# A block-diagonal spectrum stored with the frequency innermost: contiguous evictions, strided weight loads

## Chip, cores, metric

One core of one Trainium2 chip. The metric is device time in microseconds (us) of one execution. The granted clock is the share of TensorE's full clock that the throttle granted, as the profile records it. The experiments ran on two chips on which the kernel before takes about 7346 us instead of the 7284 of the result (whose chip is not on record); so experiments are compared by their ratio to the kernel before in the same rounds.

## The reference, cut to what matters

```python
def reference(x, conv_weight, ty, tx, pole1, pole2, residue):   # x: 16 x 16 x 256 x 256, fp32
    x = x + conv3x3(gn(x), conv_weight)          # circular convolution
    v = gn(x)
    alpha = fft2(v)                              # over rows, then columns
    S = einsum('ikpq,oikp,xikq->oxik', residue, A, Bm)     # a 16 x 16 matrix per frequency
    r1 = einsum('biox,oxik->bkox', alpha, S)     # mixing of channels at each frequency
    return x + ifft2(r1).real + transient(alpha, pole1, pole2, residue)
```

All arithmetic is fp32. The kernel writes the transforms as matmuls and uses that the input is real: 129 of 256 rows of the spectrum, in 33 groups of four rows (the last has one).

## The kernel before

Stage 2 works through the 33 groups. For each it transforms the rows along x (`forward`), copies the result out of PSUM into the block-diagonal tile `abd` (such a copy is called an eviction), makes the mixing matrices (`weights`, into `sg`), mixes (`mix`), and transforms back (`backward`). The parts that the change and the argument touch:

```python
    px = p2.enter_context(tc.tile_pool(name="p_x", bufs=2, space=PSUM))
    ...
    # Normalised spectrum, block diagonal in the group's rows: [(s, i, ri), fx, (s', b)]
    abd = big.tile([P, N, SB], FP, name="abd", tag="abd")        # P=128, N=256, SB=64
    ...
    def forward(g):
            ...
            for b in range(0, BQ, 2):
                ps = px.tile([P, 2, N], FP, name="ps_x", tag="ps_x")
                ... 8 fp32 matmuls into ps[:m, bb]                                # L556
                for s in range(nf):
                    rows = slice(32 * s, 32 * s + 32)
                    at = s * B + b0 + b
                    o = abd[rows, :, at : at + 2].rearrange("p n b -> p b n")
                    if s % 2:
                        nc.scalar.copy(o, ps[rows])                               # L569
                    else:
                        nc.vector.tensor_copy(o, ps[rows])                        # L571
    def weights(g):
            ...   # L629 matmuls into ps_s; copies into sg, L638 (DVE) and L640 (ACT)
            o = sg[:m, :, 2 * k : 2 * k + 2].rearrange("p n r -> p r n")
    def mix(g):
        for f0 in range(0, P, 16):
            ps = pm.tile([P, 16, 2 * C], FP, name="ps_mix", tag="ps_mix")
            for j in range(16):
                for xc in range(2):
                    f = xc * P + f0 + j
                    nc.tensor.matmul(                                             # L656
                        ps[64 * xc : 64 * xc + r, j],
                        lhsT=abd[:m, f, :r],
                        rhs=sg[:m, f],
                        start=True, stop=True)
    def backward(g):
            ...   # transposes L684 of yt[:, :, 2 * k + ro], matmuls L700, copies
```

The two values of `xc` write partitions 0 and 64, and in the trace their matmuls start in pairs, some 7 ns apart; I call them the two column halves of the array. An fp32 matmul of the mixing is recorded as two matmul instructions, each with its own weight load (in the 32 full groups, 8192 matmuls as 16384 of each), so the 256 frequencies of a group are 512 loads of 64 columns.

Of the kernel before, what the change touches and what calls it, by code (L numbers as in the profile page):

```python
# [10 lines left out]
FP = mybir.dt.float32  # L11
# [4 lines left out]
DRAM = bass.MemoryType.DRAM  # L16

C = 16  # channels, in and out
N = 256  # image side
P = 128  # L20
NT = 43  # blocks of 6 output rows; the last one starts at row 250
NPAIR = 22
NFY = 129  # rows of the half spectrum
PAD = 1024  # floats between the groups of a DRAM scratch, off a pitch of a power of two
# [4 lines left out]
def conv_then_laplace_kernel(ctx: ExitStack, tc: tile.TileContext, a: dict, out: bass.AP):  # L29
    """x1 = x + conv3x3(gn(x)); out = x1 + laplace(gn(x1)).  # L30

    1a  per image: group norm of x, the circular 3x3 convolution with the residual in its centre
        tap, statistics of the sum v; beside it the tables that depend on poles and residues
    1b  per image: gn(v), its Fourier transform along y, and its projections on the poles
    2   per 4 rows of the half spectrum: transform along x, mixing of channels per frequency,
        transform back along x
    3   per image: transform back along y, plus the transient part, plus v
    """
# [13 lines left out]
    tabs = cp.tile([P, 2, 2, N], FP, name="tabs", tag="tabs")  # cos | sin, row halves, columns  # L52
# [12 lines left out]
    # Rows padded by 64, which keeps its pitch off a power of two.  # L65
# [4 lines left out]
    # omega = 2 pi k / (n d), for the columns k of krow etc.  # L70
# [6 lines left out]
    rd = cp.tile([P, 2], FP, name="rd", tag="rd")  # 1 / (n d), along y and along x  # L77
# [8 lines left out]
    vmr = tp.tile([P, 2, B, C], FP, name="vmr", tag="vmr")  # 1/std and -mean/std of v  # L86
# [3 lines left out]
    # ---------------------------------------------------------------- 1a  # L90
# [25 lines left out]
    def sqrt_eps(sd, var, eps, tmp):  # L116
        """sd = sqrt(var + eps), var overwritten with var + eps; one Newton step."""
        nc.vector.tensor_scalar(var, var, eps, None, ALU.add)
        nc.scalar.activation(sd, var, AF.Sqrt)
        nc.vector.reciprocal(tmp, sd)  # L120
        nc.vector.tensor_tensor(tmp, tmp, var, ALU.mult)
        nc.vector.tensor_tensor(sd, sd, tmp, ALU.add)
        nc.vector.tensor_scalar(sd, sd, 0.5, None, ALU.mult)

    def group_sums(st, n, wt, gmat, tag):
        """Weighted sums over a partition's rows: of values, the group mean, of squares about it."""
        f = st.rearrange("p t (h s) -> p t h s", s=3)
        mean, m2 = f[:, :, :, 1], f[:, :, :, 2]
        tmp = sp.tile([P, NPAIR, 2], FP, name=f"tmp{tag}", tag=f"tmp{tag}")[:n]
        dev = sp.tile([P, NPAIR, 2], FP, name=f"dev{tag}", tag=f"dev{tag}")[:n]  # L130
        s = sp.tile([P, 4], FP, name=f"sum{tag}", tag=f"sum{tag}")[:n]
        nc.vector.tensor_tensor(tmp, mean, wt[:, 0], ALU.mult)
        nc.vector.tensor_reduce(s[:, 0:1], tmp, AX.XY, ALU.add)
        ps = pst.tile([P, 32], FP, name="ps_stat", tag="ps_stat")
        nc.tensor.matmul(ps[:n, 0:1], lhsT=gmat, rhs=s[:, 0:1], start=True, stop=True)
        nc.vector.tensor_copy(s[:, 1:2], ps[:n, 0:1])
        nc.vector.tensor_scalar(dev, mean, s[:, 1:2], None, ALU.subtract)
        nc.vector.tensor_tensor(dev, dev, dev, ALU.mult)
        nc.vector.tensor_tensor(dev, dev, wt[:, 0], ALU.mult)
        nc.vector.tensor_tensor(tmp, m2, wt[:, 1], ALU.mult)  # L140
        nc.vector.tensor_tensor(tmp, tmp, dev, ALU.add)
        nc.vector.tensor_reduce(s[:, 2:3], tmp, AX.XY, ALU.add)
        return s
# [83 lines left out]
    # Tables of the poles and residues, in steps between the images.  # L227
    def make_hat(side):
        """hat[t, i, (k, p, ri)]: transform of 1 / (i omega - pole) from frequencies to places."""
# [6 lines left out]
        for cc in (slice(0, n // 2), slice(n // 2, n)):  # L236
            pb = sw.tile([P, n // 2, 2], FP, name="s_pb", tag="s_a")
            nc.sync.dma_start(out=pb, in_=a[f"pole{side + 1}"][cc].partition_broadcast(P))
            for h in range(2):
                w, r = im[h][:, cc], re[h][:, cc]  # L240
                den = sw.tile([P, n // 2], FP, name="s_den", tag="s_b")
                nc.vector.tensor_scalar(w, pb[:, :, 1], -1.0, kcol[:, h : h + 1], ALU.mult, ALU.add)
                nc.gpsimd.tensor_tensor(den, w, w, ALU.mult)
                nc.gpsimd.tensor_tensor(r, pb[:, :, 0], pb[:, :, 0], ALU.mult)
                nc.gpsimd.tensor_tensor(den, den, r, ALU.add)
                nc.vector.reciprocal(den, den)
                # minus the real part, and the imaginary part
                nc.gpsimd.tensor_tensor(r, pb[:, :, 0], den, ALU.mult)
                nc.vector.scalar_tensor_tensor(w, w, -1.0, den, ALU.mult, ALU.mult)
# [4 lines left out]
        for yc in range(2):  # L254
            yy = slice(yc * P, yc * P + P)
            for half in range(2):
                cc = slice(half * 512, half * 512 + 512)
                for ri in range(2):
                    ps = psu.tile([P, 512], FP, name="ps_setup", tag="ps_setup")
                    for h in range(2):  # L260
                        # re: cos Re + sin Im;  im: cos Im - sin Re
                        first, second = ((neg, im), (im, re))[ri]
                        nc.tensor.matmul(
                            ps, lhsT=cosT[:, h, yy], rhs=first[h][:, cc], start=h == 0, stop=False
                        )
                        nc.tensor.matmul(
                            ps, lhsT=sinT[:, h, yy], rhs=second[h][:, cc], start=False, stop=h == 1
                        )
                    nc.scalar.copy(hv[:, yc, cc, ri], ps)

    def make_coef():
        """coef[(k, q, r), i, (k', p, s)]: what the products of parts r and s count in the residue
        sum's real and imaginary part, zero unless k = k'."""
# [17 lines left out]
    def make_exps(which):  # L291
        """e[(.., ri), i, t] = exp(pole t), for the poles along y with the imaginary part negated."""
# [30 lines left out]
    def make_c_start():  # L323
        """c[(i, p, ri), set, k, x]: sum over q of residue / (i omega - pole2) / 2, and in set 1 the
        conjugate of the same at -x."""
# [69 lines left out]
    # ---------------------------------------------------------------- 1b  # L395
# [15 lines left out]
    for b in range(B):  # L411
# [71 lines left out]
        # rows re: (re, im) of the sum; rows im: (-im, re)  # L483
# [9 lines left out]
    # ---------------------------------------------------------------- 2  # L493
# [19 lines left out]
    pimS = kp.tile([P, 2, C], FP, name="pimS", tag="pimS")  # imaginary parts, and conjugated  # L513
# [4 lines left out]
    # minus the real parts, on the rows re and on the rows im  # L518
# [5 lines left out]
    # Normalised spectrum, block diagonal in the group's rows: [(s, i, ri), fx, (s', b)]  # L524
    abd = big.tile([P, N, SB], FP, name="abd", tag="abd")
# [5 lines left out]
    def forward(g):  # L531
        """Transform of the group's rows along x into abd."""
        nf = 4 if g < 32 else 1
        m = nf * 32
        for b0 in range(0, B, BQ):
# [14 lines left out]
            for b in range(0, BQ, 2):  # L550
# [13 lines left out]
                for s in range(nf):  # L564
                    rows = slice(32 * s, 32 * s + 32)
                    at = s * B + b0 + b
                    o = abd[rows, :, at : at + 2].rearrange("p n b -> p b n")
# [5 lines left out]
    def weights(g):  # L573
        """s[(s, i, ri), fx, (k, ro)]: the channels' mixing at the group's frequencies."""
# [8 lines left out]
        for st in range(2):  # L583
# [9 lines left out]
            # rows re: Re and Im of 1 / (i omega - pole1); rows im: -Im and Re  # L593
# [49 lines left out]
    def mix(g):  # L643
        """y[(fx half, s, b), fx, (k, ro)] = sum over i."""
# [6 lines left out]
# [4 lines that stand above are left out]
# [3 lines left out]
                        lhsT=abd[:m, f, :r],  # L658
# [13 lines left out]
    def backward(g):  # L672
        """Transform back along x, into wD."""
# [3 lines left out]
        for k0 in range(0, C, 4):  # L677
            wo = wop.tile([P, 4, N], FP, name="wo", tag="wo")
            for k1 in range(0, 4, 2):
                # [fx, k, fx half, ro, (s, b)]  # L680
# [6 lines left out]
                # (re, im), and (-im, re) for the sines  # L687
# [24 lines left out]
            for ro in range(2):  # L712
                # The imaginary parts of rows 0 and 128 count nothing: row 128 takes that place.
# [22 lines left out]
    # ---------------------------------------------------------------- 3  # L736
# [51 lines left out]
def _constants():  # L788
    """Tables that depend on shapes alone."""
# [56 lines left out]
def _laid_out(x, L0_conv_weight, L1_conv_ty, L1_conv_tx, L1_conv_weights_pole1, L1_conv_weights_pole2, L1_conv_weights_residue):  # L846
    """The inputs in the layouts that the program reads."""
    g = {"x": np.asarray(x), "ty": np.asarray(L1_conv_ty), "tx": np.asarray(L1_conv_tx)}
    w = np.asarray(L0_conv_weight)  # co, ci, 3, 3
    band = np.zeros((8, C, 3, 6, C), w.dtype)  # L850
    for yo in range(6):
        for jy in range(3):
            # out row yo takes in row yo + 2 - jy of the block with its halo
            band[yo + 2 - jy, :, :, yo, :] = w[:, :, jy, :].transpose(1, 2, 0)
# [11 lines left out]
    # (k, q, r), i, p  # L866
    g["res_kq"] = np.repeat(rs.transpose(1, 3, 0, 2, 4).reshape(64, C, 4, 2), 2, 0)
    # (i, p, r), k, q
# [3 lines left out]
    # (r, c, p), i and (c, q, r), i  # L872
# [20 lines left out]
```

## Time and profile before

| | before |
|---|---|
| time, median of 4 | 7283.7 us (7280.2 to 7292.5) |
| mean granted TensorE clock | 0.938 |
| stage 2, first L556 to last L700 | 3727 us |
| mixing L656, start to start | 29.2 ns per instruction, 58.4 ns per pair of halves |
| recorded wait of ps_x (L556) on the ACT copy | 98.9 us |

The rows of the groups are quoted in the prediction below. They read: line, engine, operation, target and sources, number of instructions, then busy time in us and mean ns of one, then the idle time of the engine just before them and who ended it.

### The profile page before, as it was taken

What the parts mean: (1) busy time and instruction counts of PE and PEld (TensorE: products, weight loads), DVE (VectorE), ACT (ScalarE), POOL (GpSimd) and SP (SyncE); (2) the same over time, 40 slices, a digit from 0 to 9 for tenths busy, and PEclk for the clock granted to TensorE, in tenths of its full rate; (3) what the DMA queues carried; (4) which work ended last, traced back from release to release, by engine and by line L of the source; (5) the groups of instructions that cost most, each with busy time, mean ns of one, the idle gap of its engine ahead of it and who ended that gap; (6) DMA issues with size and microseconds to landing.
All of it is one profiled execution on the core that took longest, in us unless ns stands there. A gap on an engine that the chain in (4) does not pass through costs nothing.

```text
span 7295.4 us, 99265 instructions
## 1 busy us (share of the span) xinstructions
PE 6262.9 (86%) x41824; PEld 4914.9 (67%) x41824; DVE 2863.8 (39%) x5620; ACT 1845.7 (25%) x2602; POOL 984.8 (13%) x1259
## 2 busy tenths in 40 slices
PE   4876777786776776999999999999999999999999
PEld 1322222266666665888888888888888888868888
DVE  3576666433333334343333433433334334322222
ACT  2233223211111112232232332322323323211111
POOL 1211111000000002121221211212112112100000
PEclk9988888898888888999999999999999999999999
DMA  8677777746656653111111111111111111137777
GB/s 108 100 123 120 117 113 119 112 106 111 110 104 109 111 93 81 34 36 44 36 39 39 36 44 36 36 43 34 42 38 36 44 33 39 27 127 261 262 262 235
DMA packets 459980, 655.84 MB, mean 90 GB/s; under 512 B 34576, under 2 KB 347920, under 8 KB 459152
## 3 DMA queue, kind: packets, MB, share of 16 engines
q1 hardware_dynamic: 359184, 470.16, 31.0%
q0 software_dynamic: 32768, 112.21, 7.7%
q10 hardware_dynamic: 67584, 67.12, 2.6%
q8 instruction: 331, 5.42, 0.3%
q14 instruction: 113, 0.93, 0.0%
HBM read 372.05 MB, written 277.35 MB: 89 GB/s over the span
## 4 chain that ended last, share of the span: by engine, by line
PE 65%; DMA 13%; DVE 11%; ACT 5%; SPq 4%; issue 1%; POOL 1%; ACTq 0%; DVEq 0%; POOLq 0%
PE ps_inv L700 13%; PE ps_s L629 10%; PE ps_x L556 8%; PE ps_mix L656 7%; PE ps_conv L191 5%; PE ps_dft L434 5%; DMA xt<-in_x 4%; DMA x1nD<-gat 4%; ACT abd L569 3%; DVE abd L571 3%; PE ps_f L778 3%; PE ps_f L777 3%; PE ps_f L776 3%; DMA vD<-vt 3%; PE ps_dft L442 3%; SPq L470 2%
## 5 line engine op out<-in xcount | busy, mean ns | idle before, releaser
L556 PE MATMUL ps_x<-tabs,t 128*128 128x256 f32 (+1 forms) x4224 | 980.7, 385 | 141.0 <-ACT abd L569 98.9
L700 PE MATMUL ps_inv<-tabs,tr 128*128 128x256 f32 (+1 forms) x4224 | 1043.2, 400 | 16.9 <-DVE tr L694 11.7
L191 PE MATMUL ps_conv<-xt,wband 128*96 128x512 f32 (+1 forms) x1408 | 712.0, 623 | 302.6 <-ACT vt L198 278.5
L556 PEld LDWEIGHTS ps_x<-tabs,t 128*128 128x128 f32 (+1 forms) x4224 | 767.8, 188 | 294.1 <-ACT abd L569 140.5
L629 PE MATMUL ps_s<-ct,ab 128*128 128x256 f32 (+1 forms) x4224 | 929.5, 380 | 9.6 <-ACT sg L640 9.6
L700 PEld LDWEIGHTS ps_inv<-tabs,tr 128*128 128x128 f32 (+1 forms) x4224 | 800.9, 195 | 179.9 <-ACT tr L692 41.0
L629 PEld LDWEIGHTS ps_s<-ct,ab 128*128 128x128 f32 (+1 forms) x4224 | 789.2, 188 | 140.0 <-issue 21.2
L571 DVE COPY abd<-ps_x 32x512 f32<-32x512 f32 x520 | 535.4, 1030 | 434.7 <-ACT abd L569 241.5
L191 PEld LDWEIGHTS ps_conv<-xt,wband 128*96 128x96 f32 x1408 | 238.6, 174 | 683.8 <-issue 360.8
L569 ACT COPY abd<-ps_x 32x512 f32<-32x512 f32 x512 | 529.5, 1034 | 578.6 <-DVE abd L571 576.1
L656 PE MATMUL ps_mix<-sg,abd 128*64 128x32 f32 (+1 forms) x16896 | 540.9, 223 | 61.3 <-DVE sg L638 59.3
L613 POOL TENSOR_TENSOR ab<-uv,kmask 128x512 f32<-128x512 f32 x512 | 542.6, 1061 | 357.9 <-PE ps_s L629 313.5
L656 PEld LDWEIGHTS ps_mix<-sg,abd 128*64 128x64 f32 (+1 forms) x16896 | 515.4, 137 | 111.4 <-DVE sg L638 62.6
L434 PE MATMUL ps_dft<-fy,vy 128*128 128x258 f32 x2048 | 562.6, 399 | 8.5 <-DVE vy L421 8.5
L454 PE MATMUL psd<-gs,hat 128*128 128x128 f32 x1024 | 225.0, 311 | 305.3 <-DVE gs L452 305.3
L638 DVE COPY sg<-ps_s 128x512 f32<-128x512 f32 (+1 forms) x264 | 273.7, 1037 | 496.4 <-PE ps_s L629 495.5
L548 POOL COPY t<-t 128x256 f32<-128x256 f32 (+1 forms) x264 | 111.1, 453 | 2571.7 <-PE ps_x L556 2105.8
L449 ACT COPY gat<-ps_dft 128x258 f32<-128x258 f32 x512 | 195.2, 384 | 1033.0 <-PE ps_dft L442 758.1
L198 ACT ACTIVATE vt<-ps_conv,sumx 96x512 f32<-96x512 f32 x352 | 224.1, 670 | 772.5 <-DMA vD<-vt 418.4
L640 ACT COPY sg<-ps_s 128x512 f32<-128x512 f32 (+1 forms) x264 | 277.5, 1051 | 541.1 <-PE ps_s L629 540.3
L779 DVE TENSOR_TENSOR ol<-ps_f,vl 128x512 f32<-128x512 f32 x256 | 176.9, 692 | 601.6 <-PE ps_f L778 595.0
L454 PEld LDWEIGHTS psd<-gs,hat 128*128 128x128 f32 x1024 | 175.3, 209 | 341.7 <-DVE gs L452 324.0
(177 smaller groups left out, 6848.6 us busy)
## 6 DMA issues: line engine op xcount, KB each, us to landing
vy<-vD SPq DMA_DIRECT2D x128, 512.0 KB, 5.6
x1D<-gat SPq DMA_DIRECT2D x32, 2048.0 KB, 25.0
t<-x1D SPq DMA_DIRECT2D x256, 256.0 KB, 3.3
wl<-wD SPq DMA_DIRECT2D x128, 512.0 KB, 4.8
vl<-vD POOLq DMA_DIRECT2D x128, 512.0 KB, 8.1
out_y<-ol ACTq DMA_DIRECT2D x128, 512.0 KB, 9.1
wD<-wo SPq DMA_DIRECT2D x252, 256.0 KB, 3.2
vD<-vt SPq DMA_DIRECT2D x80, 768.0 KB, 4.7
```

The lines of the kernel that those rows point to most:

```text
L191: nc.tensor.matmul(ps[:, :m], lhsT=wc if tap == 1 else wband[:, tap, :], rhs=t[:, t0 + j : t0 + j + m, 2 - tap : 2 - tap + N], start=tap == 0,
L434: nc.tensor.matmul(ps[:, 0 : 2 * NFY], lhsT=vy[:, h, j, xx], rhs=fy[:, h], start=h == 0, stop=h == 1,)
L454: nc.tensor.matmul(psd[:, j], lhsT=hat[1][:, xc, i], rhs=gs[:, xc], start=xc == 0, stop=xc == 1)
L556: nc.tensor.matmul(ps[:m, bb], lhsT=t[:, xc, b + bb, :m], rhs=tab[:, xc], start=n == 0, stop=n == 3,)
L569: nc.scalar.copy(o, ps[rows])
L571: nc.vector.tensor_copy(o, ps[rows])
L613: nc.gpsimd.tensor_tensor(ab.rearrange("p a s i r -> p (a s) i r"), uv[:, k].rearrange("p t o s r -> p (t o s) r").unsqueeze(2).to_broadca ...
L629: nc.tensor.matmul(ps[:m, ro], lhsT=ab[:, 2 * st + ro, :nf].rearrange("p s i r -> p (s i r)"), rhs=ct[:, st, k], start=st == 0, stop=st == 1,)
L638: nc.vector.tensor_copy(o, ps[:m])
L640: nc.scalar.copy(o, ps[:m])
L656: nc.tensor.matmul(ps[64 * xc : 64 * xc + r, j], lhsT=abd[:m, f, :r], rhs=sg[:m, f], start=True, stop=True,)
L700: nc.tensor.matmul(ps[: 2 * r, kk], lhsT=t[:, kk, xc], rhs=tab[:, xc], start=n == 0, stop=n == 3,)
```

## The change

The intent: write `abd` with the frequency innermost, so that an eviction writes 256 contiguous floats per image instead of single floats 256 bytes apart. The price: the 64 weight columns of a mixing matmul are then 1024 bytes apart. Comments were dropped as well, which changes nothing that runs.

```diff
-    # Normalised spectrum, block diagonal in the group's rows: [(s, i, ri), fx, (s', b)]
-    abd = big.tile([P, N, SB], FP, name="abd", tag="abd")
+    abd = big.tile([P, SB, N], FP, name="abd", tag="abd")
...
-                    o = abd[rows, :, at : at + 2].rearrange("p n b -> p b n")
+                    o = abd[rows, at : at + 2]
...
-                        lhsT=abd[:m, f, :r],
+                        lhsT=abd[:m, :r, f],
```

## The prediction

> **What bounds the kernel now.** I read the page first, for the stretch in which the changed tile lives. The changed tile, abd, exists only in stage 2 (33 groups: transform along x, mixing, transform back).
>
> ```profile
> PE 6262.9 (86%) x41824; PEld 4914.9 (67%) x41824; DVE 2863.8 (39%) x5620; ACT 1845.7 (25%) x2602; POOL 984.8 (13%) x1259
> ...
> PE   4876777786776776999999999999999999999999
> ```
>
> From about slice 16 on TensorE is at 90% or more. Starts of L569 in the trace put stage 2 from about 2770 to 6470 us, one full group every 110.6 us; in the window 2760 to 6475 us TensorE is busy 3503.6 of 3715 us, DVE 1412.7, ACT 1097.4. So DVE and ACT seconds are nearly free here; only what holds TensorE counts.
>
> Next, the groups that touch abd, and the waits list for TensorE:
>
> ```profile
> L571 DVE COPY abd<-ps_x 32x512 f32<-32x512 f32 x520 | 535.4, 1030 | 434.7 <-ACT abd L569 241.5
> ...
> L569 ACT COPY abd<-ps_x 32x512 f32<-32x512 f32 x512 | 529.5, 1034 | 578.6 <-DVE abd L571 576.1
> L656 PE MATMUL ps_mix<-sg,abd 128*64 128x32 f32 (+1 forms) x16896 | 540.9, 223 | 61.3 <-DVE sg L638 59.3
> ```
>
> ```profile
> PE ps_x L556 <- ACT abd L569: 98.9, 96, 2.9
> ```
>
> The evictions of ps_x cost 535 + 530 us of DVE and ACT, but TensorE stands still for them only 98.9 us in the whole run. The timeline of one group shows how:
>
> ```profile
> 4344.55 7.17 PE L556 MATMUL ps_x<-tabs,t 128*128 128x256 f32 x32 [1.34 <-ACT abd L569]
> ...
> 4348.31 1.03 DVE L571 COPY abd<-ps_x 32x512 f32<-32x512 f32 x1 [1.69 <-PE ps_x L556]
> 4349.37 1.02 ACT L569 COPY abd<-ps_x 32x512 f32<-32x512 f32 x1 [1.68 <-DVE abd L571]
> 4350.42 1.02 DVE L571 COPY abd<-ps_x 32x512 f32<-32x512 f32 x1 [1.09 <-ACT abd L569]
> ...
> 4351.48 1.04 ACT L569 COPY abd<-ps_x 32x512 f32<-32x512 f32 x1 [1.09 <-DVE abd L571]
> ...
> 4352.58 0.70 PE L556 MATMUL ps_x<-tabs,t 128*128 128x256 f32 x2 [0.86 <-ACT abd L569]
> ```
>
> The four evictions of one ps_x tile run strictly one after another, DVE, ACT, DVE, ACT, 4.2 us from 4348.31 to 4352.52. There are two ps_x buffers. A tile is 16 matmul instructions at 216 ns (start to start) = 3.46 us. The third tile needs the first tile's buffer, so each two tiles cost TensorE 0.86 us of standing.
>
> [...] The kernel before writes abd with 256 bytes between neighbouring elements[...] the copies of wo, which have the same shape and a contiguous target, take 679 and 575 ns instead of 1030 and 1034.
>
> ```profile
> L709 DVE COPY wo<-ps_inv 32x512 f32<-32x512 f32 x4 | 2.7, 679 | 13.4 <-PE ps_inv L700 13.4
> ...
> L711 ACT COPY wo<-ps_inv 32x512 f32<-32x512 f32 x4 | 2.3, 575 | 16.5 <-PE ps_inv L700 16.5
> ```
>
> [...] the transposes L684 take as weights every 32nd float of yt [...]:
>
> ```profile
> 4318.28 0.61 PE L684 MATMUL ps_tr<-ident,yt 128*128 128x128 f32 x4
> ...
> 4328.16 11.39 PE L656 MATMUL ps_mix<-sg,abd 128*64 128x32 f32 x384
> ```
>
> One such matmul is 275 ns long, so four in 0.61 us start (610 - 275) / 3 = 110 ns apart: 128 columns of strided weights fit in 110 ns, 0.86 ns a column or less. [...] If the weight port suffered as DVE does, the loads would take over 200 ns each and show.
>
> **The change, part by part.**
> Removed: the stride of the abd writes. I take 680 ns for DVE and 580 for ACT, from the wo copies. Off DVE 520 x 350 ns = 182 us, off ACT 512 x 454 ns = 232 us. This is beside TensorE's work and counts nothing by itself. The order of instructions and their waits is unchanged on every engine (the ACT copy still waits for the DVE copy of the same tile), so the chain stays serial: 2 x (0.68 + 0.58) + three gaps of 0.05 = 2.7 us instead of 4.2. That is under the 3.46 us that the other buffer's tile takes, so the wait of L556 on L569 should vanish: 98.9 us. The similar short wait of L629 behind the ACT queue at the end of the transform (9.6 us in its row) should go too, since ACT is no longer behind. Sum 108 us; I count 102, for first tiles and leftovers.
> Not touched: the 216 ns cadence of L556, L629 and L700, and the wait of the first mixing matmuls on the last sg eviction (59 us), which hangs on DVE's table work and not on abd.
> Added: the mixing loads 64 weight columns that lie 1024 bytes apart, where they were 256 contiguous bytes. There are 16,384 loads in the full groups. The cadence now is (11.39 - 0.22) / 383 = 29.2 ns per instruction, 58.4 ns for a pair (one for each half of the array's columns; the pairs start together). [...] so I take the pair to be bound by two loads running side by side, each at the rate that the strided transposes also reach. By that reading a stride costs nothing: 0 us.
> Sum: 7284 - 102 = 7182 us, 1.4% faster.
>
> **The rivals.**
> *A: the weight port pays for the stride.* For: a DVE reduction that reads single elements 1024 bytes apart pays just as the 256-byte writes do, while one that reads pairs doesn't:
>
> ```profile
> L476 DVE TENSOR_REDUCE acc<-prod 128x64 f32<-128x2048 f32 x32 | 71.5, 2276 | 0.0
> ...
> L363 DVE TENSOR_REDUCE s_c<-s_w 128x256 f32<-128x1024 f32 x16 | 30.6, 1914 | 0.0
> ```
>
> About 1.7 ns per element for L363 (after some 160 ns of fixed time) against 1.04 for L476. And the transposes prove only one stream at 128 bytes; in the mixing two streams run at once, at 1024 bytes, and the two together could be limited to what one reaches. [...] Against: the transposes' 110 ns, and that DVE pays the same 1.7 ns at 128 (sg), 256 (abd) and 1024 bytes, so the size of the stride seems not to matter[...].
> *B: a half-sized penalty.* [...]
> *C: the eviction gain is taken by another wait,* for example ps_x waiting for the copies of t on POOL and DVE. The POOL copies start as soon as a buffer is free and need 1.4 us of a 6.9 us period, so I expect little; at worst the time stays at 7284.
>
> **Range and chances.** No penalty (with C's shades) I hold at 62%: 7165 to 7290. A at about 30%, 7550 to 7640, or far beyond in a few cases; B at 8%. Over 2% faster needs 146 us, more than all the waits found: 4%. So 7185 us, range 7165 to 7640, which is wide because the cases lie apart: faster 0.04, same 0.61, slower 0.35.
>
> **What would show it.** Right: abd copies at about 680 and 580 ns; L556's wait on L569 near zero; mixing cadence still 29 ns; the group's period down from 110.6 to about 107.5 us. Wrong: a mixing cadence above 30 ns per instruction[...], with L656 then the longest line of TensorE; or the wait of L556 renamed to POOL, DVE or a DMA.

What is cut rested on figures that no trace of this case shows, terms of the rivals among them: A came to 7621 us and B to about 7380. The traces alone give A about 110 ns a pair, an estimate: 64 columns at L363's 1.7 ns, or two loads in turn at the 0.86 ns a column of the transposes, about 423 us more ((110 - 58.4) x 8192). They give B about 84 ns a pair, also an estimate: 29.2 ns for a matmul and 55 for 64 columns at 0.86. The 160 ns of fixed time are an estimate too (DVE copies of 128 and 512 elements a partition take 289 and 692 ns, L452 and L667, so 1.05 ns an element and some 155 ns), and so is "over 200 ns" a load (128 columns at 1.7 ns are 218).

## More of the kernel before

One caution that matters later: matmuls are pipelined. An L556 matmul is recorded as 379 ns long, while the next starts after 216 ns. The granted clock of TensorE in 40 slices of the run, in tenths, for comparison with the page after:

```profile
PEclk9988888898888888999999999999999999999999
```

## The result, and the profile after

The changed kernel takes 7909.5 us (median of 4, 7902.0 to 7913.5) against 7283.7: 8.5% slower, ratio 1.0854 with a 95% interval of 1.0838 to 1.0869. A ratio here is the mean time of one kernel's fast runs over that of the other's fast runs of the same rounds, so not quite the ratio of the medians.

The page of the changed kernel: engines, clock by slices, and the groups that answer to those quoted above.

```profile
PE 7001.7 (88%) x41824; PEld 5687.2 (72%) x41824; DVE 2724.0 (34%) x5620; ACT 1615.7 (20%) x2602; POOL 991.8 (13%) x1259
...
PEclk9988888888888788989898989898989888989999
...
L656 PE MATMUL ps_mix<-sg,abd 128*64 128x32 f32 (+1 forms) x16896 | 1252.0, 321 | 60.0 <-DVE sg L638 59.0
...
L571 DVE COPY abd<-ps_x 32x512 f32<-32x512 f32 x520 | 355.2, 683 | 472.8 <-PE ps_x L556 383.4
...
L569 ACT COPY abd<-ps_x 32x512 f32<-32x512 f32 x512 | 295.3, 577 | 790.6 <-DVE abd L571 789.7
```

The evictions did what was hoped: 1030 to 683 ns on DVE, 1034 to 577 on ACT. But L656 is now the costliest line of TensorE, 1252.0 us busy instead of 540.9, and the granted clock dips again and again.

The waits, same row as before (total us, times, longest):

```profile
PE ps_x L556 <- ACT abd L569: 1.7, 2, 1.1
```

The wait that the change was to remove is gone. In its place, here is one long mixing stretch and the matmuls that follow it, in the timeline:

```profile
4301.40 28.21 PE L656 MATMUL ps_mix<-sg,abd 128*64 128x32 f32 x384
4329.55 5.67 PE L556 MATMUL ps_x<-tabs,t 128*128 128x256 f32 x14
```

384 instructions took 11.39 us before and take 28.21 us now. After them 14 matmuls of L556 take 5.67 us, about 405 ns each where 216 is usual. The windows of the same stretch show the clock (columns: window, length, then busy us and count of PE, PEld, DVE, ACT, POOL, then clock, DMA share, GB/s):

```profile
4301.50:4306.00 4.50, 4.50 (x64) 4.50 (x64) 0.69 (x1) 0.00 (x0) 0.00 (x0) 1.00 0.47 119
4308.00:4329.00 21.00, 21.00 (x294) 21.00 (x292) 1.38 (x2) 1.19 (x2) 0.00 (x0) 0.50 0.01 2
4329.60:4335.00 5.40, 5.40 (x16) 4.36 (x15) 1.97 (x3) 1.15 (x2) 0.00 (x0) 0.56 0.00 0
```

and the mixing stretch of the kernel before, for comparison:

```profile
4328.20:4339.50 11.30, 11.30 (x386) 11.26 (x385) 2.08 (x3) 1.76 (x3) 0.00 (x0) 1.00 0.20 51
```

Two things are to be seen. TensorE counts as 100% busy in every window, and yet the granted clock falls to 0.50 after some 6 us of the slow mixing (1.00 up to 4305.5, 0.90 in the next 2 us, 0.50 from 4307.5 on). And the mixing isn't slow because of that clock: 64 instructions in 4.50 us at clock 1.00 are 70 ns each, 294 in 21 us at clock 0.50 are 71 (the counts take in those that straddle an edge; from start to start it is 73). The half clock costs only what comes next, the first ps_x matmuls (405 ns each, at clock 0.56).

### The profile page after: what moved, and what is told of

Same layout as the page of the kernel before. It is cut to its first block, busy times and chain, and to the rows that moved or that the text cites. A ratio compares the mean times of both kernels' runs of the same rounds, so it can differ in the third digit from the quotient of the medians.

```text
span 7911.7 us, 99265 instructions
## 1 busy us (share of the span) xinstructions
PE 7001.7 (88%) x41824; PEld 5687.2 (72%) x41824; DVE 2724.0 (34%) x5620; ACT 1615.7 (20%) x2602; POOL 991.8 (13%) x1259
## 4 chain that ended last, share of the span: by engine, by line
PE 75%; DMA 13%; DVE 6%; SPq 3%; ACT 1%; issue 1%; POOL 1%; ACTq 0%; DVEq 0%; POOLq 0%
PE ps_mix L656 16%; PE ps_inv L700 12%; PE ps_x L556 12%; PE ps_s L629 10%; PE ps_dft L434 4%; PE ps_conv L191 4%; DMA x1nD<-gat 4%; DMA xt<-in_x 3%; DMA vD<-vt 3%; PE ps_f L778 3%; PE ps_f L777 3%; PE ps_f L776 3%; PE ps_dft L442 2%; PE psd L454 2%; DMA vy<-vD 2%; DVE xst L159 1%
## 5 line engine op out<-in xcount | busy, mean ns | idle before, releaser
L656 PEld LDWEIGHTS ps_mix<-sg,abd 128*64 128x64 f32 (+1 forms) x16896 | 1225.9, 244 | 110.2 <-DVE sg L638 62.4
L656 PE MATMUL ps_mix<-sg,abd 128*64 128x32 f32 (+1 forms) x16896 | 1252.0, 321 | 60.0 <-DVE sg L638 59.0
L700 PE MATMUL ps_inv<-tabs,tr 128*128 128x256 f32 (+1 forms) x4224 | 1050.7, 402 | 7.9 <-ACT tr L692 4.7
L556 PE MATMUL ps_x<-tabs,t 128*128 128x256 f32 (+1 forms) x4224 | 1017.8, 398 | 43.9 <-DMA t<-x1D 39.4
L556 PEld LDWEIGHTS ps_x<-tabs,t 128*128 128x128 f32 (+1 forms) x4224 | 821.4, 198 | 176.6 <-issue 42.4
L700 PEld LDWEIGHTS ps_inv<-tabs,tr 128*128 128x128 f32 (+1 forms) x4224 | 804.5, 196 | 171.0 <-ACT tr L692 39.8
L629 PE MATMUL ps_s<-ct,ab 128*128 128x256 f32 (+1 forms) x4224 | 922.2, 379 | 0.0
L629 PEld LDWEIGHTS ps_s<-ct,ab 128*128 128x128 f32 (+1 forms) x4224 | 791.8, 188 | 120.5 <-POOL ab L613 1.3
L571 DVE COPY abd<-ps_x 32x512 f32<-32x512 f32 x520 | 355.2, 683 | 472.8 <-PE ps_x L556 383.4
L569 ACT COPY abd<-ps_x 32x512 f32<-32x512 f32 x512 | 295.3, 577 | 790.6 <-DVE abd L571 789.7
L667 DVE COPY yt<-ps_mix 128x512 f32<-128x512 f32 (+1 forms) x136 | 94.0, 691 | 958.5 <-PE ps_mix L656 850.9
L434 PEld LDWEIGHTS ps_dft<-fy,vy 128*128 128x128 f32 x2048 | 374.1, 204 | 43.0 <-issue 9.6
```

The lines of the kernel that those rows point to most:

```text
L434: nc.tensor.matmul(ps[:, 0 : 2 * NFY], lhsT=vy[:, h, j, xx], rhs=fy[:, h], start=h == 0, stop=h == 1,)
L556: nc.tensor.matmul(ps[:m, bb], lhsT=t[:, xc, b + bb, :m], rhs=tab[:, xc], start=n == 0, stop=n == 3,)
L629: nc.tensor.matmul(ps[:m, ro], lhsT=ab[:, 2 * st + ro, :nf].rearrange("p s i r -> p (s i r)"), rhs=ct[:, st, k], start=st == 0, stop=st == 1,)
L656: nc.tensor.matmul(ps[64 * xc : 64 * xc + r, j], lhsT=abd[:m, :r, f], rhs=sg[:m, f], start=True, stop=True,)
L700: nc.tensor.matmul(ps[: 2 * r, kk], lhsT=t[:, kk, xc], rhs=tab[:, xc], start=n == 0, stop=n == 3,)
```

## The experiments

**Theories.** *Line* (the expectations' name for it): what costs is that the weight columns lie 16 bytes or more apart, at whatever distance, while columns in pairs, 8 bytes apart, don't pay. *Distance*: columns 1024 bytes apart collide because of the power of two. *Two streams*: one load pays nothing, the two halves loading at once do. And for the split of the total: evictions alone, loads alone, or only both together.

**e1_evictions_alone and e2_loads_alone** split the change into its halves. They read the same memory through another view, so that evictions and loads have the pattern of different layouts. Their outputs are wrong, which doesn't matter for the times. All waits stay.

```diff
 # e1, from the changed kernel
-                        lhsT=abd[:m, :r, f],
+                        lhsT=abd.rearrange("p s n -> p (s n)")[:m, f * SB : f * SB + r],
 # e2, from the kernel before
-                        lhsT=abd[:m, f, :r],
+                        lhsT=abd.rearrange("p n s -> p (n s)")[:m, f : f + (r - 1) * N + 1 : N],
```

> The changed kernel with the mixing reading 64 contiguous floats of the same tile (another view of the same memory, so the result is wrong on purpose). Evictions contiguous, weight loads contiguous. If the eviction half of the prediction holds, abd copies take 680 and 580 ns, the wait of ps_x on the ACT copy falls from 98.9 us to under 5, the mixing stays at 29 ns an instruction at full clock, and the time is 7284 - 102 = about 7180 us (ratio to before 0.986). If the slowdown of the changed kernel came from the evictions (for instance ACT and DVE freed earlier collide with something), this run is slower than before too.

> The kernel before with the mixing taking every 256th float of the same tile as its weights (wrong on purpose). Evictions strided, weight loads strided. If the strided loads alone are the cause, the mixing runs at about 73 ns an instruction, the granted clock falls to a half during its long stretch, the wait of ps_x on ACT stays near 99 us less what a cold array hides, and the time is about the changed kernel's 7910 plus the 100 us that its evictions saved, about 8000 us (ratio 1.10). If the two parts only hurt together, it stays under 7500.

e1: 7191.0 us, ratio 0.9788 (0.9772 to 0.9804). e2: 8046.7 us, ratio 1.0948 (1.0932 to 1.0965). The mixing of e1 and e2, by form:

```profile
L656 PE MATMUL ps_mix<-sg,abd 128*64 128x32 f32 x16384 | 528.2, 223 | 58.4 <-DVE sg L638 58.0 <-ACT tr L692 0.2
```

```profile
L656 PE MATMUL ps_mix<-sg,abd 128*64 128x32 f32 x16384 | 1236.0, 323 | 58.7 <-DVE sg L638 58.5 <-ACT tr L692 0.2
```

The strided loads alone make the slow mixing; evictions are not needed for it. The eviction half alone is worth 2.1%, more than the 1.4% that I had predicted. The two don't simply add: 0.979 x 1.095 = 1.072, where both together gave 1.085. Beside the slow loads the evictions are worth less, (1.0948 - 1.0854) x 7347 = 69 us instead of 157. Of the 88 us of difference 54 are found at L629, most of them in one wait: at the start of a group, TensorE waits after two L629 matmuls for a ps_x buffer. L629 takes 971 us from start to start before, 912 in e1, and already 917 in e2, although e2's evictions are slow. It fits that the ps_x matmuls after a mixing stretch run "cold" there, at about half clock, as in the changed kernel (405 ns each at 0.56), so that the evictions keep up with them; no run tests it.

**e4_probe** measures loads by themselves: the kernel before, followed by blocks of 128 fp32 matmuls with a given step between weight columns.

```diff
+    for halves, ncol, mov, steps in ((2, 64, 32, (1, 2, 4, 8, 32, 256, 257, 260, 1)),
+            (1, 64, 32, (1, 2, 4, 32, 256)), (0, 128, 32, (1, 2, 4, 32, 136)), (0, 128, 128, (1, 4, 32, 136))):
+        ...
+                nc.tensor.matmul(ps[h : h + ncol, o : o + mov],       # h: 0 and 64 in turn if halves == 2
+                    lhsT=wq[:, f * 4 : f * 4 + (ncol - 1) * st + 1 : st], rhs=mq[:, :mov], start=True, stop=True)
```

> The kernel before with a probe after its end: blocks of 128 fp32 matmuls with weights of a given step, 64 columns on alternating halves of the array, 64 columns on one half, 128 columns, and 128 columns with 128 moving columns. Theory line: steps of 4, 8, 32, 256, 257, 260 floats all cost about 73 ns an instruction on alternating halves, steps 1 and 2 cost 29. Theory distance: only step 256 costs 73, steps 257 and 260 and 4 to 32 cost 29 to 40. Theory two streams: on one half or on the whole array the step costs nothing (128 columns at 110 ns an instruction at every step, as the transposes of this kernel suggest). [...]

Start to start, per instruction: on one half at 64 columns, 58.3 ns at step 1, 60.2 at step 2 (8 bytes), 118.5 at step 4 (16 bytes), 110.4 at 32 and 110.6 at 256. So one load by itself pays at 16 bytes and more, and the distance hardly matters. (Steps 1 and 2 ran at clock 1.00, the other three almost wholly at 0.50; that the clock is not the reason is shown by e6 below.) On alternating halves, steps 4 to 260 gave 55 to 60 ns, not the 73 of the changed kernel; the repeat of step 1 ended at 29.1. Full loads of 128 columns with 128 moving columns took 111.7 ns at step 1 (end of the block) and 233.5, 219.6 and 238.3 at steps 4, 32 and 136, at a granted clock of 1.00. The clock spoils much of the rest: the first blocks, and those of 128 columns with 32 moving, ran at 0.50, where contiguous loads are slow too (53 ns on alternating halves, 213 ns for 128 columns). Open after it: where the changed kernel's 73 ns come from, and why its transposes show 110 ns.

**e6_probe** repeats this with a warm-up of 24 full matmuls before each block, with the addresses of the real mixing, and with transposes. Its edit is shortened here to the blocks and their addresses.

```diff
+        for j in range(24):   # warm-up
+            nc.tensor.matmul(warm, lhsT=wq[:, j * P : j * P + P], rhs=mq[:, :256], start=True, stop=True)
+   # (block, first weight column for frequency p and half x, step); x * 128 floats apart are 512 bytes
+        ("q_real", x * P + p, 256)        ("q_fixed_moving", the same, one moving operand throughout)
+        ("q_halves_near", x * 4 + p, 256) ("q_halves_same", p, 256) ("q_halves_odd", x * 132 + p, 256)
+        ("q_contiguous", (x * P + p) * 64, 1)   ("q_pairs", .., 2)   ("q_fours", .., 4)
+        ("q_one_real", p, 256, one half)  ("q_full_contiguous", 128 columns, 1) ("q_full_strided", 128 columns, 32)
+        ("q_transpose_contiguous", 1) ("q_transpose_strided", 32) ("q_transpose_far", 136)
```

> The kernel before with a second probe after its end, each block of 128 fp32 matmuls after a warm-up of full matmuls, so that the clock starts at full speed. q_real repeats the addresses of the changed mixing: 73 ns an instruction if addresses make the difference to the 56 to 60 ns of the first probe, 56 if something else in the kernel does. If the moving operand is the reason, q_fixed_moving falls to 56; if the 512 bytes between the halves' weights are, q_halves_near, q_halves_same or q_halves_odd do. q_contiguous 29, q_pairs 30, q_fours about 59 (line) or 29 (distance). q_one_real: 110 or more if each half pays by itself, 58 if only the two together do. Plain full loads: contiguous 110, strided 215 to 235 also at the start of the block, while the clock is still full (line); or 110 there (the clock alone was the reason in the first probe). Transposes: 110 ns at every step if a transpose loads its weights in another way than a matmul, which is my explanation for the misleading 110 ns; 215 in a long row of them if four were too few to show it.

Groups of this probe, 256 matmul instructions each (128 for a transpose); the busy time over the number is the time of one, give or take 2 ns:

```profile
L801 PE MATMUL q_full_strided<-mq,wq 128*128 128x128 f32 x256 | 56.3, 382 | 0.0
L801 PE MATMUL q_full_contiguous<-mq,wq 128*128 128x128 f32 x256 | 28.7, 275 | 0.0
...
L801 PE MATMUL q_one_real<-mq,wq 128*64 128x32 f32 x256 | 28.5, 293 | 0.0
...
L801 PE MATMUL q_real<-mq,wq 128*64 128x32 f32 x256 | 18.9, 327 | 0.0
L801 PE MATMUL q_fixed_moving<-mq,wq 128*64 128x32 f32 x256 | 18.9, 327 | 0.0
L801 PE MATMUL q_halves_same<-mq,wq 128*64 128x32 f32 x256 | 18.9, 326 | 0.0
...
L801 PE MATMUL q_fours<-mq,wq 128*64 128x32 f32 x256 | 15.6, 298 | 0.0
...
L812 PE MATMUL q_transpose_strided<-ident,wq 128*128 128x128 f32 x128 | 14.6, 276 | 0.0
...
L801 PE MATMUL q_halves_near<-mq,wq 128*64 128x32 f32 x256 | 14.5, 291 | 0.0
L801 PE MATMUL q_halves_odd<-mq,wq 128*64 128x32 f32 x256 | 14.4, 290 | 0.0
...
L812 PE MATMUL q_transpose_contiguous<-ident,wq 128*128 128x128 f32 x128 | 14.1, 273 | 0.0
...
L801 PE MATMUL q_pairs<-mq,wq 128*64 128x32 f32 x256 | 7.9, 224 | 0.0
```

From the starts of the instructions, the same as time per instruction:

| block | ns | what it says |
|---|---|---|
| contiguous / pairs (8 bytes) | 29.2 / 30.0 | columns 8 bytes apart cost nothing to speak of |
| fours (16 bytes) | 59.9 | columns 16 bytes apart double it, though they are close: *line*, not *distance* (12 bytes were not tried, so where between 8 and 16 the cost begins is not measured) |
| one half, 1024 bytes | 110.5 | one stream alone pays; a half's load takes 58.3 without the stride (e4): not *two streams* |
| both halves, 1024 bytes, 16 or 528 bytes between the halves | 55.5, 55.3 | the halves overlap fully: 111 ns a pair |
| the real addresses: 512 bytes between the halves | 72.8 | 146 ns a pair, as in the changed kernel |
| the same with 0 bytes between, or with one moving operand | 72.7, 72.8 | neither makes a difference; the moving operand has no part in it |
| 128 columns, contiguous / 128 bytes | 111.7 / 219.2 | a full load pays too, with the clock at 1.00 throughout (28 and 55 us of windows) |
| transpose, contiguous / 128 / 544 bytes | 109.2 / 112.5 / 112.2 | a transpose does not pay |

The clock doesn't explain the slow blocks, although it fell to 0.50 after some 5 us of each block with a stride of 16 bytes or more on 64 columns (mean 0.63 over 18.5 us of *real*, 0.59 over 28 us of one half): *real* takes 72.3 ns in its first quarter, at 1.00, and 73.9 in its last, at 0.50; one half takes 110.7 and 110.3. Contiguous loads slow down instead, from 29 to 53 ns (e4). So at a clock of 0.50 a stride of 16 bytes costs little, 59.2 ns against 53.2 on alternating halves. What makes the clock fall isn't shown; slow loads alone don't: with 128 strided columns and 128 moving, at 219.2 ns an instruction, it stayed at 1.00. The strided loads take 1.7 ns a column (110.5 / 64, 219.2 / 128), as long as the prediction estimated for a DVE element 128 to 1024 bytes from the next; whether for the same reason isn't shown.

So the line theory holds for the weights of plain matmuls, at the steps tried (8 bytes cost next to nothing, 16 to 1040 about double), and a second cost sits on top: with a step of 1024 bytes, two halves whose columns are 0 or 512 bytes apart slow each other from 111 to 146 ns a pair. The cause isn't shown, only that 16 bytes more between them remove it.

**e5_fours and e7_padded** ask the same in the real kernel, in one run each.

```diff
 # e5 and e3 (q = 4 and 2), from the changed kernel
-    abd = big.tile([P, SB, N], FP, name="abd", tag="abd")
+    abd = big.tile([P, N // q, SB, q], FP, name="abd", tag="abd")
-                    o = abd[rows, at : at + 2]
+                    o = abd[rows, :, at : at + 2].rearrange("p h b j -> p b h j")    # ps read as "p b (h j)"
-                        lhsT=abd[:m, :r, f],
+                        lhsT=abd[:m, f // q, :r, f % q],
 # e7, from the changed kernel
-    abd = big.tile([P, SB, N], FP, name="abd", tag="abd")
+    abd = big.tile([P, SB, N + 4], FP, name="abd", tag="abd")                        # written in [.., :N]
```

> abd as [group of four frequencies, (s, b), 4]: evictions write runs of four floats, weight columns lie 16 bytes apart[...]. Theory line[...]: the mixing is slow, 59 to 73 ns an instruction, the clock falls, time 7750 to 7950 us. Theory distance (1024 bytes apart is the trouble): mixing at 29 to 31 ns, time about 1.9% under before, like the pairs.

> The changed kernel with rows of 260 floats instead of 256, so weight columns are 1040 bytes apart. Theory line: nothing to gain, mixing stays between 59 and 73 ns an instruction, time 7750 to 7950. Theory power of two (columns 1024 bytes apart collide): mixing falls to 30 ns, time like the pairs. If only the excess over the first probe's 56 to 60 ns comes from the power of two, mixing falls to about 60 and the time to about 7700.

e5: 7781.3 us in one run beside 7348.4 for the kernel before, e7: 7769.5. Groups of e5, then of e7:

```profile
L656 PE MATMUL ps_mix<-sg,abd 128*64 128x32 f32 x16384 | 1038.9, 298 | 58.2 <-DVE sg L638 58.0 <-ACT tr L692 0.2
```

```profile
L656 PE MATMUL ps_mix<-sg,abd 128*64 128x32 f32 x16384 | 1029.3, 297 | 58.8 <-DVE sg L638 58.6 <-ACT tr L692 0.2
```

Both mix at 58 to 60 ns an instruction inside a stretch, twice the kernel before. Columns 16 bytes apart are no better than 1040: distance is out. The padding takes away the excess of 1024 over the other steps (some 210 us of L656) and no more.

**e3_pairs** is the layout that the line theory recommends: columns in pairs 8 bytes apart, runs of two floats on the write side (diff above, q = 2).

> abd laid out as pairs of neighbouring frequencies, [frequency pair, (s, b), 2]: evictions write runs of two floats (512 bytes apart), weight columns lie 8 bytes apart[...]. Theory line[...]: both are at full speed, evictions 690 and 590 ns, mixing 29 ns, about 7180 us, 1.4% faster than before. Theory distance[...]: mixing also fast. Rival: any stride other than 4 bytes costs the weight port, mixing above 40 ns. If the eviction only speeds up for long runs, copies stay at 1030 ns and the time is that of before.

7211.7 us, correct, ratio 0.9813 (0.9798 to 0.9828): 1.9% faster than before. Its groups:

```profile
L656 PE MATMUL ps_mix<-sg,abd 128*64 128x32 f32 x16384 | 541.0, 225 | 58.4 <-DVE sg L638 57.8 <-issue 0.4 <-ACT tr L692 0.2
...
L571 DVE COPY abd<-ps_x 32x512 f32<-32x512 f32 x520 | 355.6, 684 | 414.6 <-PE ps_x L556 321.8 <-ACT abd L569 86.1
...
L569 ACT COPY abd<-ps_x 32x512 f32<-32x512 f32 x512 | 303.4, 593 | 645.3 <-DVE abd L571 644.6
```

Runs of two floats are as good as runs of 256 for DVE (684 ns against 683), and 16 ns off for ACT (593 against 577).

**e8_order, e10_order_again** keep the layout of the kernel before and change only the order in which an eviction walks it: both images of a frequency, then the next frequency. The writes come in runs of two, and the jump is moved to the PSUM side.

```diff
-                    o = abd[rows, :, at : at + 2].rearrange("p n b -> p b n")
+                    o = abd[rows, :, at : at + 2]
-                        nc.scalar.copy(o, ps[rows])
+                        nc.scalar.copy(o, ps[rows].rearrange("p b n -> p n b"))
-                        nc.vector.tensor_copy(o, ps[rows])
+                        nc.vector.tensor_copy(o, ps[rows].rearrange("p b n -> p n b"))
```

> The layout of the kernel before, with the evictions walking both images of a frequency before the next frequency: writes come as runs of two floats, 256 bytes apart, and reads of the PSUM tile alternate between places 1024 bytes apart. If [...] PSUM reads don't care, copies take 690 and 590 ns, the mixing stays at 29 ns, and the time is like the pairs or 12 us better, 1.9 to 2.1% under before. If PSUM reads pay for the jump, copies stay at 1000 ns or more and the time is that of before within 0.5%.

> e8_order again, on the same chip as its neighbours: ratio to before 0.979 as then, PSUM reads not penalised.

e8: 7192.9 us, correct, ratio 0.9793 (0.9775 to 0.9811). e10: 7196.1 us, 0.9794 (0.9777 to 0.9811). PSUM reads that alternate between places 1024 bytes apart cost nothing (the copies take 684 and 593 ns, as in e3, which reads PSUM in order), and the weights stay contiguous. Of e10:

```profile
L571 DVE COPY abd<-ps_x 32x512 f32<-32x512 f32 x520 | 355.7, 684 | 416.8 <-PE ps_x L556 323.9 <-ACT abd L569 86.0
...
L569 ACT COPY abd<-ps_x 32x512 f32<-32x512 f32 x512 | 303.4, 593 | 648.3 <-DVE abd L571 647.5
```

This is all of the change's gain without its cost.

**e9_order_both** does the same for the copies into `sg`, whose writes were single floats 128 bytes apart.

```diff
-            o = sg[:m, :, 2 * k : 2 * k + 2].rearrange("p n r -> p r n")      # and ps[:m] read as "p r n -> p n r"
+            o = sg[:m, :, 2 * k : 2 * k + 2]
```

> The order of e8_order used for the evictions of sg too (runs of two floats, 128 bytes apart, PSUM read alternating). [...] the sg copies fall from 1037 and 1052 ns to about 690 and 590. They stand before TensorE only where the first mixing matmuls wait for the last sg copy (58 us in 32 groups), and that wait hangs mostly on the table work ahead of it on DVE; I expect 10 to 15 us of it back, so 0.1 to 0.2% better than e10_order_again. If the interval of the two overlaps fully, the sg copies don't count.

7174.0 us, correct, ratio 0.9769 (0.9753 to 0.9785), the fastest of all; its interval overlaps with that of e10. The groups of e9:

```profile
L638 DVE COPY sg<-ps_s 128x512 f32<-128x512 f32 x256 | 175.1, 684 | 565.2 <-PE ps_s L629 565.2
...
L640 ACT COPY sg<-ps_s 128x512 f32<-128x512 f32 x256 | 156.0, 609 | 616.9 <-PE ps_s L629 616.2
```

1037 and 1052 ns became 684 and 609, and the wait of the first mixing matmuls on the last sg copy fell from 59 to 48 us. The copies hardly stood in TensorE's way, so little came of it. In the traces stage 2 of e9 is 26 us shorter than that of e10: 10 us are this wait, and 10 more lie among the L700 matmuls.

**e11_after_again** puts the changed kernel on the same chip as e10, which differs from it in the weight loads alone.

> The changed kernel again, on the same chip as e10_order_again, which has the same fast evictions and contiguous weight loads. Ratio to before 1.085. Against e10_order_again the whole difference is the weight loads and what follows from them: about 700 us in the mixing (16,384 x 43 ns), about 60 us in the cold ps_x matmuls after each mixing stretch, and nothing over 20 us in any other line of TensorE.

7970.3 us, ratio 1.0849 (1.0833 to 1.0865). Start-to-start time of TensorE by line, from the two traces:

| line | e10 | e11 | difference |
|---|---|---|---|
| L656 mixing | 541.2 | 1239.9 | +698.7 |
| L556 ps_x (slow after the mixing) | 943.0 | 998.4 | +55.4 |
| L700 ps_inv | 1036.9 | 1057.9 | +21.0 |
| L629 ps_s | 912.3 | 912.3 | 0.0 |
| stage 2 | 3572.1 | 4347.6 | +775.5 |

The first three lines make up the whole difference of stage 2. The 21 us of L700 are intervals of over 420 ns (216 of them against 119), where matmuls meet a half clock (in the trace after, 12 of them from 4388.9 us on take 4.54 us, with the clock at 0.58); there are such in the kernel before as well (213), so I don't put them down to the mixing with certainty.

## Why the prediction was wrong

- **The bound and the path**: right. TensorE is the bound of stage 2 (busy 3503.6 of 3715 us before), and the time of DVE and ACT counted only where it held a PSUM buffer.
- **Evictions at 680 and 580 ns, wait of L556 on L569 near zero**: right, 683 and 577 ns, 98.9 us down to 1.7.
- **The worth of the evictions, 102 us**: right in kind, too small. Alone they bring 7347.6 - 7191.0 = 157 us (e1), and 150 us in e10. I had summed the recorded idle times, which count from the end of a matmul's record, 379 ns after its start, although the next could have started after 216. Every stall is recorded about 160 ns short (379 - 216), and stalls below that not at all. From the starts, the intervals over 232 ns between matmuls of L556 and L629 exceed 216 ns by 157 us in sum in the kernel before and by 16 us in e1, so 141 us, where the idle columns showed 108. The traces (of different chips) differ by another 25 us among the L700 matmuls, of which 213 intervals are over 420 ns before and 101 in e1; why fewer meet the half clock there isn't shown. So 157 us is also more than the 146 that the prediction called more than all the waits found.
- **"By that reading a stride costs nothing: 0 us"**: this is the step that failed. It carried over to the mixing what the transposes L684 show, 128 columns in 110 ns at a stride of 128 bytes. The measurement was right (112.5 ns in a long row, e6), but a plain matmul pays where a transpose doesn't: 219.2 ns strided against 111.7 contiguous for 128 columns at the same 128 bytes. In the mixing the pair of halves went from 58.4 to 146 ns, and the line cost 699 us more instead of 0.
- **Two loads side by side, one in each half, bound the pair**: right. One half alone needs 58.3 ns a load, two halves 58.4 a pair, so the halves run side by side; and when a half's load became slower (110.5 ns), the pair did too (111). So the mixing was bound by its loads, and each ns on a load came straight onto the path. Rival B, loading and computing in turns, is out: that would be about 42 ns an instruction (half of the 84 estimated above) where 73 were measured. Nor does it fit 128 contiguous columns with 128 moving in 111.7 ns (e6): 128 moving columns alone need about 108, an estimate from L556's 216 ns for 256, which leaves no time for a load in turn.
- **Rival A, weight loads pay for the stride**: right that they pay (e6: 110.5 ns a load on one half against 58.3), and given 30%. Its size, 7621 us in all, was not: the 110 ns a pair estimated above are what e6 finds when the halves lie 16 or 528 bytes apart (111 ns, so 52.6 x 8192 pairs = 431 us more), but the real addresses cost 146. That is about 35 ns x 8192 pairs = 287 us more, which with the 431 makes 718 (measured 699: the average pair over all of e11's mixing took 145 ns, e10's 60). It also missed the clock, which cost some 55 to 60 us in the ps_x matmuls after each stretch. Measured: +699 for the mixing, +55 for the ps_x matmuls, against e10.
- **The range** ended at 7640 because A was its upper mode with nothing on top. The text named the case that both costs come together and left it outside.
- **Rival C, another wait**: didn't come. TensorE's waits on DVE and DMA in stage 2 stayed as they were or fell (first mixing on sg 59.3 to 59.0 us, ps_x on the DMA of t 39.2 to 39.4, ps_inv on L694 11.7 to 3.2), and none on POOL came up.

In sum for the result: -150 for the evictions (e10), +699 and +55 to +60 for loads and clock, some 20 for L700, make about +626, and 7909.5 - 7283.7 = 626 was measured. The terms come from other chips than the total, so the agreement to the last figures is partly luck.

What stays open: why a transpose is exempt, and why the halves slow each other. The runs show both effects (112.5 ns against 219.2, 146 ns a pair against 111), not their cause. Whether the transpose's strided tensor goes in as weights at all is untested. The trace lists `ident,yt` in the order moving, weights, as for the plain matmuls, but no run checks it.

## What to carry to other kernels

Before trading a strided write for a strided read, ask which side has slack and whether each side meets its elements at least in pairs: runs of two floats were enough here for the writes (684 and 593 ns against 1030 and 1034), columns 8 bytes apart for the loads (30.0 ns an instruction against 59.9 at 16 bytes). Look first for an order of walking that gives both sides their pairs: changing the order of the copies alone (two `rearrange`s) took all of the gain (ratio 0.979), while the change cost 8.5%; the layout in pairs did nearly as well (0.981, and the intervals overlap). And take evidence for a cost from the same kind of instruction: a transpose was no stand-in for a matmul's weight load (112.5 ns against 219.2), and the recorded idle time of the pipelined TensorE was not the whole stall (108 us against 141).
